# Moving input transposes between VectorE and TensorE in a fused attention and mixture-of-experts kernel

## The chip, the core and the metric

The kernel runs on one core of one Trainium2 chip. The metric is the device time of one execution in microseconds; the shown time is the median of three runs.

## The reference

The program computes one cross-attention layer and one mixture-of-experts layer over 4096 tokens of width 256, both with a residual. Cut to what matters:

```
x = x + xattn(ctx, layernorm(x), fside, fside, ...)      # 16 heads, 77 context rows
xn = layernorm(x)
probs = softmax(xn @ Wr)                                  # 9 experts
topk_w, topk_idx = top_k(probs, 2); topk_w /= sum(topk_w)
gate   = silu(xn @ Wg[e])                                 # 256 -> 704
hidden = gate * (xn @ Wu[e])
x = x + sum over the token's two experts e of topk_w[e] * (hidden @ Wd[e])   # 704 -> 256
```

## The kernel before

The program has two stages. The attention stage walks over 32 tiles of 128 tokens (i = 0 to 31 in the long loop that holds `scores`, `exponentials`, `weights_turn`, `values`). While it does so, the routing of each finished group of four tiles is worked out and every token is written with its weight into the list of each expert that it chose (`list_d` in DRAM).

The expert stage then walks over blocks of gathered tokens, all of one expert. A pair block has 256 tokens, a single block 128; a flex block is a single one whose two halves belong to two experts. There are 41 blocks, numbered j = 0 to 40: blocks 0 to 5 are early pairs (`EARLY = 6`), whose lists are complete before the last group is routed; from block 6 on a pair and a single alternate (blocks 6 to 35; the singles 9, 15, 21 and 27 are flex blocks, the other eleven are not), and blocks 36 to 40 are pairs. A further flex block, the rare one, has number 41 (`NBLK`) and is computed behind block 36 (`RARE_AT`) inside a `tc.If` on a count read from the routing; its products are skipped when the count is small, but its two additions to the output are always issued.

Engines run in the order in which the program lists their instructions; the kernel has switched to a manual order. For block j the loop issues:

- `fetch()`: SyncE loads the weights of block j+2 (`weights`, six transfers per expert); GpSimd gathers the token numbers of a later block (`tokens`, tile `ids`) and the rows of block j+2 (`inputs`, tile `yin`, an indirect DMA for each 128 rows; three `yin` buffers).
- the gate and up products. In a pair (`hidden_pair`) TensorE makes six chunks `pg`, f = 0 to 5, of 128 hidden units each (44 matmuls of 256 columns); ScalarE takes the silu of each (`sl`), VectorE multiplies (`hid`, L1249 and L1252). In a single (`hidden_one`) TensorE makes `psg`, `psu` and `psb` with the tokens as the stationary operand, ScalarE takes the silu, VectorE multiplies (`hs`, L1285 to L1290).
- the transposes of block j+1's rows from `yin` to `xT`, on VectorE: `turning` (L1215) has 16 instructions for a block, each of which turns a strip of 32 partitions in squares of 32 by 32. `advance(upcoming, 4)` issues four of them behind each chunk f = 1 to 4 of a pair; in a single all 16 stand behind the last `hs` multiplication. Blocks 0 and 1 are turned by TensorE instead (`turn`, L1228: four 128 by 128 transposes into PSUM tile `px`, and a copy by ScalarE, L1231).
- `down(j-1)`: TensorE multiplies the hidden units of the block before with `wd` (12 matmuls for each 128 tokens; 24 with half the columns for a flex block), VectorE scales by the routing weights (`co`, L1321).
- `adding(j-1)`: GpSimd adds the rows to the output by indirect DMA (L1353). Additions of different blocks may touch the same rows, so each waits until the ones before have landed; the two of a pair are declared independent.
- in a single, `hidden_turn`: TensorE turns `hs` (`ph`, six transposes), ScalarE and VectorE copy to `hid`.

During blocks 0 to 4, VectorE also finishes the routing of the last group and plans the later blocks; `pump()` issues up to six of these small instructions behind each chunk f of a pair. GpSimd writes the last group's list entries (L950, eight indirect DMAs) once VectorE has worked out their places (`r_pli`, L948).

At the head of the attention stage, two leftover pieces of a folded weight (`fill(left[...])`: TensorE products `pu`, L746, with one copy to `u` on ScalarE, L142, and one on VectorE, L140) are issued in steps i = 1 and i = 2, behind the third `scores`.

Of the kernel before, what the change touches and what calls it, by code (L numbers as in the profile page):

```python
# [21 lines left out]
def kernel(  # L22
# [231 lines left out]
    def scores(i, k):  # L254

        zT = zTs[i]
        h, n = banks[k]
        if k == 0:
            nmx[i] = stat.tile([P, H], F32, tag="mx", name=f"mx{i}")
        psc = pscs[k] = ps_sc.tile([P, TB], F32, tag=f"sc{k}", name=f"psc{i}_{k}")  # L260
        w = n * J + (E if h + n == H else 0)
        for c in range(C):
            nc.tensor.matmul(  # L263
                psc[:, :w], zT[:, c, :], g_sb[i // NS // GPB][:, c, h * J : h * J + w],
                start=(c == 0), stop=(c == C - 1),
            )
        nc.vector.tensor_reduce(  # L267
            nmx[i][:, h : h + n], psc[:, : n * J].rearrange("p (h j) -> p h j", h=n), AX.X,
            ALU.max, negate=True,
        )  # L270

    def exponentials(i, k):
        h, n = banks[k]
        if k == 0:
            exs[i] = pools["qpool"].tile([P, H, J], F32, tag="ex", name=f"ex{i}")
        for q in range(n):
            nc.scalar.activation(  # L277
                exs[i][:, h + q, :], pscs[k][:, q * J : (q + 1) * J], AF.Exp,
                bias=nmx[i][:, h + q : h + q + 1],
            )  # L280
# [75 lines left out]
    with ExitStack() as kvs:  # L356
# [436 lines left out]
        def fill(*what, new=mm_tile):  # L793

            for b, n in what:
                first_keys(b, n, new)
# [438 lines left out]
    def hidden_pair(j, also={}, upcoming=iter(())):  # L1235

        (w,), xT, hid = wgus.pop(j), xTs.pop(j), hids[j % 2]
        for f in range(NF + 1):
            pg = mm_tile(f"pg{j}_{f}").rearrange("p (g t) -> p g t", g=2)
            for g, at in enumerate((f * P, UP[f]) if f < NF else (f * P,)):  # L1240
                for c in range(C):
                    nc.tensor.matmul(  # L1242
                        pg[:, g, :], w[:, c, at : at + P], xT[:, c, :],
                        start=(c == 0), stop=(c == C - 1),
                    )
            sl = pools["spool"].tile([P, TS], F32, tag="sl", name=f"sl{j}_{f}")
            if f < NF:
                nc.scalar.activation(sl, pg[:, 0, :], AF.Silu)  # L1248
                nc.vector.tensor_tensor(hid[:, f, :], pg[:, 1, :], sl, ALU.mult)  # L1249
            else:  # L1250
                nc.scalar.activation(sl[64:128, :], pg[0:64, 0, :], AF.Silu)
                nc.vector.tensor_tensor(  # L1252
                    hid[64:128, NF, :], pg[64:128, 0, :], sl[64:128, :], ALU.mult
                )
            pump()
            if f:
                advance(upcoming, 4)
            for fn in also.get(f, ()):
                fn()
# [5 lines left out]
        n = P // len(of_experts)  # L1265
        return [slice(h * n, (h + 1) * n) for h in range(len(of_experts))]

    def hidden_one(j):


        ws, xT = wgus.pop(j), xTs.pop(j)
        hs = hss[j] = late["hs"] if j >= NBLK else pools["spool"].tile(
            [P, FF], F32, tag="hs", name=f"hs{j}", bufs=1
        )
        pgs = {}
        for k, (at, n) in (("g", (0, FA)), ("u", (FF + FB, FA)), ("b", (FA, 2 * FB))):
            pgs[k] = mm_tile(f"ps{k}{j}")
            for c in range(C):
                for w, rows in zip(ws, lanes(ws)):
                    nc.tensor.matmul(  # L1280
                        pgs[k][rows, :n], xT[:, c, rows], w[:, c, at : at + n],
                        start=(c == 0), stop=(c == C - 1),
                    )
        nc.scalar.activation(hs[:, :FA], pgs["g"], AF.Silu)
        nc.vector.tensor_tensor(hs[:, :FA], pgs["u"], hs[:, :FA], ALU.mult)  # L1285
        nc.scalar.activation(hs[:, FA:], pgs["b"][:, :FB], AF.Silu)
        nc.vector.tensor_tensor(
            hs[:, FA : NF * P], pgs["b"][:, FB + FT : 2 * FB], hs[:, FA : NF * P], ALU.mult
        )
        nc.vector.tensor_tensor(  # L1290
            hs[:, NF * P :], pgs["b"][:, FB : FB + FT], hs[:, NF * P :], ALU.mult
        )
# [139 lines left out]
    for i in range(N_SUB + 1):  # L1432
        g, s = divmod(i, NS)
        now_on = i < N_SUB
        q = g - 1

        if now_on:
            if i:
                scores(i, 0)
                exponentials(i, 0)  # L1440
            if i > 1:
                residual_stats(i - 2)
            if i:
                scores(i, 1)
            if 0 < i < N_SUB - 1:
                query(i + 1)
            if i:
                scores(i, 2)
        if i:
            if i < 3:  # L1450
                fill(left[i - 1])
            weights_turn(i - 1)
            weights_copy(i - 1, 0)
            weights_copy(i - 1, 1)
        if i == 2:
            vsides.close()
        if now_on and i:
            exponentials(i, 1)
        if 0 < i < N_SUB - 1:
            query_turn(i + 1)  # L1460
        if now_on and i:
            exponentials(i, 2)
        if i:
            weights_copy(i - 1, 2)
        if now_on:
            queries_logits(i)
            if s == 1 and q > 0:
                ranks(q - 1)
            if i == (G_EARLY + 1) * NS + 2:
                early = early_blocks()  # L1470
                advance(early, 2)
        else:
            turn(0)
            advance(chosen)
            ranks(q - 1)
            residual_stats(i - 2)
        if i:
            values(i - 1)


        if now_on and s == 0:
            if g + 1 < NG:
                for k in range(NS):
                    query_stats(g + 1, k)
            if q > 0:
                advance(chosen)
        if now_on and s == 1:
            if g + 1 < NG:
                query_variance(g + 1)
            if q >= 0:  # L1490
                advance(residual(q))
                root(q)
            if g + 1 < NG:
                query_root(g + 1)
            nc.scalar.activation(junk, eps_t, AF.Exp)
            if q > 0:
                advance(places(q - 1))
        if now_on and s == 2:
            if g + 1 < NG:
                query_scale(g + 1)  # L1500
            if q >= 0:
                advance(logits(q))
                exponential(q)
                advance(normalised(q))
            if g + 2 < NG:
                load_x(g + 2)
        if early is not None:
            if advance(early, 7):
                early = None
                now[0] = -1  # L1510
                fetch()
        if now_on and s == 3 and q >= 0:
            chosen = choices(q)
            advance(chosen, 14)
        if now_on:
            attention_weights(i)
        if i:
            attended(i - 1)
        if i == BH * GPB * NS:
            halves[0].close()  # L1520
            open_experts()
# [12 lines left out]
    for j in range(LAST):  # L1534
        now[0] = j
        if j == EARLY:
            assert not rest
            open_late()
        fetch()
        if j == EARLY + 1:  # L1540
            count = nc.values_load(
                tabs["flex_total"][0:1, 0:1], min_val=0, max_val=2 * FLEX
            )
        if j == RARE_AT - 1:
            tokens(NBLK)
            inputs(NBLK)
        if j == RARE_AT:
            weights(NBLK)
            weights_upper(NBLK)
        upcoming = turning(j + 1) if j else iter(())  # L1550
        if blocks[j][0] == 2:
            hidden_pair(j, upcoming=upcoming)
        else:
            hidden_one(j)
        advance(upcoming)
        if j:
            split(j + 1)
            down(j - 1)
            for r in rounds_of(j - 1):
                adding(*r)  # L1560
        if blocks[j][0] == 1:
            hidden_turn(j)
        if j == RARE_AT:
            split(NBLK)

            with tc.If(count > 2 * (FLEX - RARE)):
                turn(NBLK)
                hidden_one(NBLK)
                hidden_turn(NBLK)
                down(NBLK)  # L1570
            for r in rounds_of(NBLK):
                adding(*r)

    hidden_pair(LAST, {1: [lambda: down(LAST - 1), lambda: adding(*rounds_of(LAST - 1)[0])]})
    down(LAST)
# [34 lines left out]
```

## Time and profile before

| | us |
|---|---|
| median of three runs | 919.2 (916.86 to 920.8) |
| the profiled execution | 920.17 |
| its span | 918.4 |
| TensorE busy in the span | 894.0 (97%) |
| VectorE busy | 609.5 (66%) |
| ScalarE busy | 315.4 (34%) |
| GpSimd busy | 316.0 (34%) |
| VectorE on transposes L1215, 624 instructions | 172.5 |

The page gives busy times of each engine, the span in 40 slices, the chain that ended last, and the costliest groups of instructions by line and tile. A timeline lists instructions in the order of time: start, duration, engine, line, operation, output tile, input tiles, shape, number of merged instructions, and in brackets how long the engine had been idle and what ended that. PE is TensorE's matmul, PEld its weight load, DVE is VectorE, ACT ScalarE, POOL GpSimd.

### The profile page before, as it was taken

What the parts mean: (1) busy time and instruction counts of PE and PEld (TensorE: products, weight loads), DVE (VectorE), ACT (ScalarE), POOL (GpSimd) and SP (SyncE); (2) the same over time, 40 slices, a digit from 0 to 9 for tenths busy, and PEclk for the clock granted to TensorE, in tenths of its full rate; (3) what the DMA queues carried; (4) which work ended last, traced back from release to release, by engine and by line L of the source; (5) the groups of instructions that cost most, each with busy time, mean ns of one, the idle gap of its engine ahead of it and who ended that gap; (6) DMA issues with size and microseconds to landing.
All of it is one profiled execution on the core that took longest, in us unless ns stands there. A gap on an engine that the chain in (4) does not pass through costs nothing. (4 is left out here: it accounts for less than half of the span.)

```text
span 918.4 us, 13855 instructions
## 1 busy us (share of the span) xinstructions
PE 894.0 (97%) x4164; PEld 682.8 (74%) x4164; DVE 609.5 (66%) x1934; ACT 315.4 (34%) x1016; POOL 316.0 (34%) x328
## 2 busy tenths in 40 slices
PE   8999999999999999997999999999999999999996
PEld 6646777777777767786887777777777777778885
DVE  4776688878788887656974656656656656666551
ACT  3556566575656556441111111111111111111110
POOL 3000002130504343165345435435435435444432
PEclk9999999999999999999999999999999999999998
DMA  7001010512202700455769779879779877779722
GB/s 263 2 20 43 24 46 24 47 33 38 69 24 48 234 24 25 118 155 134 212 163 293 214 220 311 225 214 313 225 220 305 235 219 217 219 229 318 226 34 24
DMA packets 110378, 137.94 MB, mean 150 GB/s; under 512 B 24663, under 2 KB 80287, under 8 KB 110304
## 3 DMA queue, kind: packets, MB, share of 16 engines
q1 hardware_dynamic: 92746, 119.66, 41.9%
q0 software_dynamic: 17344, 17.26, 11.1%
q8 instruction: 34, 0.56, 0.3%
q14 instruction: 40, 0.33, 0.2%
q10 hardware_dynamic: 214, 0.13, 0.0%
HBM read 119.48 MB, written 18.33 MB: 150 GB/s over the span
## 5 line engine op out<-in xcount | busy, mean ns | idle before, releaser
L1242 PE MATMUL pg<-xT,wgu 128*128 128x256 f32 x1144 | 255.2, 383 | 9.1 <-issue 8.0
L1242 PEld LDWEIGHTS pg<-xT,wgu 128*128 128x128 f32 x1144 | 216.6, 191 | 43.1 <-issue 11.3
L1215 DVE STREAM_TRANSPOSE xT<-yin 32x128 f32<-32x128 f32 (+1 forms) x624 | 172.5, 276 | 18.9 <-DMA yin<-y_d,ids 9.7
L1318 PE MATMUL po<-wd,hid 128*128 128x256 f32 (+1 forms) x804 | 180.8, 380 | 0.0
L1318 PEld LDWEIGHTS po<-wd,hid 128*128 128x128 f32 (+1 forms) x804 | 149.6, 187 | 28.3 <-issue 3.7
L1353 POOL DMA_INDIRECT out_dram<-co,ids x63 | 100.7, 1599 | 176.5 <-DVE co L1321 153.1
L277 ACT ACTIVATE ex<-psc,mx 128x77 f32<-128x77 f32 x512 | 124.2, 362 | 104.1 <-DVE mx L267 98.0
L950 POOL DMA_INDIRECT list_d<-r_entry,r_pli x64 | 68.6, 1073 | 250.7 <-issue 123.5
L336 PE MATMUL po<-u,aT 128*128 128x265 f32 x640 | 151.6, 391 | 0.3
L263 PE MATMUL psc<-g,zT 128*128 128x462 f32 (+1 forms) x384 | 139.2, 511 | 0.0
L336 PEld LDWEIGHTS po<-u,aT 128*128 128x128 f32 x640 | 118.7, 189 | 23.1 <-ACT aT L325 0.9
L1248 ACT ACTIVATE sl<-pg 128x256 f32<-128x256 f32 x130 | 49.7, 384 | 230.2 <-PE pg L1242 162.9
L263 PEld LDWEIGHTS psc<-g,zT 128*128 128x128 f32 x384 | 72.3, 189 | 58.2 <-issue 50.5
L1249 DVE TENSOR_TENSOR hid<-pg,sl 128x256 f32<-128x256 f32 x130 | 55.1, 424 | 85.5 <-ACT sl L1248 67.7
L1183 POOL DMA_INDIRECT yin<-y_d,ids x67 | 70.7, 1055 | 24.2 <-issue 19.4
L297 DVE TENSOR_REDUCE sm<-ex 128x16 f32<-128x1232 f32 x32 | 45.9, 1434 | 35.3 <-ACT ex L277 32.3
L267 DVE TENSOR_REDUCE mx<-psc 128x6 f32<-128x462 f32 (+1 forms) x96 | 55.7, 581 | 18.2 <-PE psc L263 13.9
L325 ACT COPY aT<-pa 128x512 f32<-128x512 f32 (+1 forms) x96 | 49.5, 554 | 24.2 <-PE pa L317 24.2
L1321 DVE TENSOR_SCALAR co<-po,ids 128x256 f32<-128x256 f32 x67 | 30.6, 481 | 35.5 <-PE po L1318 34.8
L317 PEld LDWEIGHTS pa<-ident,an 128*128 128x128 f32 x320 | 36.7, 141 | 8.1 <-PE po L336 1.4
L317 PE MATMUL pa<-ident,an 128*128 128x128 f32 x320 | 40.3, 273 | 1.0 <-DVE an L301 1.0
L1285 DVE TENSOR_TENSOR hs<-psu,hs 128x512 f32<-128x512 f32 x15 | 10.4, 692 | 46.4 <-PE psu L1280 46.4
(312 smaller groups left out, 784.6 us busy)
## 6 DMA issues: line engine op xcount, KB each, us to landing
wgu<-in_L_ffn_Wg_dram SPq DMA_DIRECT2D x41, 704.0 KB
wd<-in_L_ffn_Wd_dram SPq DMA_DIRECT2D x41, 640.0 KB
wgu<-in_L_ffn_Wu_dram SPq DMA_DIRECT2D x41, 512.0 KB
wgu<-in_L_ffn_Wu_dram SPq DMA_DIRECT2D x41, 128.0 KB
x<-in_x_dram SPq DMA_DIRECT2D x8, 512.0 KB
out_dram<-x SPq DMA_DIRECT2D x8, 512.0 KB
y_d<-y SPq DMA_DIRECT2D x8, 512.0 KB
w<-in_L_ffn_Wg_dram SPq DMA_DIRECT2D x5, 704.0 KB
```

What stands on the lines that cost most here:

```text
L263: nc.tensor.matmul(psc[:, :w], zT[:, c, :], g_sb[i // NS // GPB][:, c, h * J : h * J + w], start=(c == 0), stop=(c == C - 1),)
L267: nc.vector.tensor_reduce(nmx[i][:, h : h + n], psc[:, : n * J].rearrange("p (h j) -> p h j", h=n), AX.X, ALU.max, negate=True,)
L277: nc.scalar.activation(exs[i][:, h + q, :], pscs[k][:, q * J : (q + 1) * J], AF.Exp, bias=nmx[i][:, h + q : h + q + 1],)
L317: nc.tensor.transpose(pa[:, q * P : (q + 1) * P], ans[i][:, (k + q) * P : (k + q + 1) * P], ident)
L336: nc.tensor.matmul(po[:, :DE], aT[:, n, :], u_sb[b][:, n, :], start=(n == 0), stop=(n == KC - 1))
L950: i = nc.gpsimd.indirect_dma_start(out=list_d[:, :], out_offset=bass.IndirectOffsetOnAxis(ap=place_i[:, s : s + 1], axis=0), in_=entries[k ...
L1183: return nc.gpsimd.indirect_dma_start(out=dst, out_offset=None, in_=src, in_offset=bass.IndirectOffsetOnAxis(ap=offsets, axis=0), **kw,)
L1215: yield nc.vector.transpose(xT[q : q + Q].rearrange("p c (h t) -> p h c t", t=P)[:, :nh, :, a : a + Q], of(yins, j)[a : a + Q].rearrange(" ...
L1242: nc.tensor.matmul(pg[:, g, :], w[:, c, at : at + P], xT[:, c, :], start=(c == 0), stop=(c == C - 1),)
L1249: nc.vector.tensor_tensor(hid[:, f, :], pg[:, 1, :], sl, ALU.mult)
L1318: nc.tensor.matmul(po[rows, :D], hid[:, f, at], d[:, f, :], start=(f == 0), stop=(f == NF))
L1353: i = nc.gpsimd.indirect_dma_start(out=out_r, out_offset=bass.IndirectOffsetOnAxis(ap=rows_of(j, h, rows), axis=0), in_=cos[j][:, h, :], i ...
```

## The change

Five edits. (1) Blocks 2 to 6 are turned by TensorE (`turn`), between the gate and up products of block j (j = 1 to 5) and `down(j-1)`; VectorE turns blocks 7 to 40. (2) In a pair, VectorE's four groups of four transposes stand behind chunks f = 2 to 5 instead of f = 1 to 4. (3) In a single, eight of the sixteen stand ahead of the `hs` multiplication with the up product, the other eight remain behind the last `hs` multiplication. (4) The rare block's two additions no longer follow block 36 directly: one stands behind block 37's addition (that of block 36), one behind block 38's. (5) The two leftover fills in steps 1 and 2 stand behind the first `scores` and ahead of the first `exponentials`.

```
@@ hidden_pair
-            if f:
+            if f > 1:
                 advance(upcoming, 4)
@@ hidden_one
-    def hidden_one(j):
+    def hidden_one(j, upcoming=iter(())):
...
         nc.scalar.activation(hs[:, :FA], pgs["g"], AF.Silu)
+
+        advance(upcoming, 8)
         nc.vector.tensor_tensor(hs[:, :FA], pgs["u"], hs[:, :FA], ALU.mult)
@@ the attention loop
             if i:
                 scores(i, 0)
+                if i < 3:
+                    fill(left[i - 1])
                 exponentials(i, 0)
...
         if i:
-            if i < 3:
-                fill(left[i - 1])
             weights_turn(i - 1)
@@ the block loop
-        upcoming = turning(j + 1) if j else iter(())
+
+        upcoming = turning(j + 1) if j >= EARLY else iter(())
         if blocks[j][0] == 2:
             hidden_pair(j, upcoming=upcoming)
         else:
-            hidden_one(j)
+            hidden_one(j, upcoming)
+        if 0 < j < EARLY:
+            turn(j + 1)
         advance(upcoming)
...
-            for r in rounds_of(NBLK):
-                adding(*r)
+            rare = rounds_of(NBLK)
+        elif j > RARE_AT and rare:
+
+            adding(*rare.pop(0))
+    assert not rare
```

## The prediction

> **What bounds the kernel now.** I read the page's first part, TensorE's waits, the timeline around them, and the windows. TensorE fills the span:
>
> ```profile
> span 918.4 us, 13855 instructions
> ...
> PE 894.0 (97%) x4164; PEld 682.8 (74%) x4164; DVE 609.5 (66%) x1934; ACT 315.4 (34%) x1016; POOL 316.0 (34%) x328
> ```
>
> 24.4 us of the span are without a matmul, so only time in which TensorE idles, runs slowed or does avoidable work can be won. The timeline of TensorE shows the largest stretch of idling, in the early pairs:
>
> ```profile
> 409.33 5.34 PE L1318 MATMUL po<-wd,hid 128*128 128x256 f32 x24
> 418.02 10.56 PE L1242 MATMUL pg<-xT,wgu 128*128 128x256 f32 x40 [3.34 <-issue]
> ...
> 436.56 9.73 PE L1242 MATMUL pg<-xT,wgu 128*128 128x256 f32 x44 [1.72 <-issue]
> ...
> 452.41 9.73 PE L1242 MATMUL pg<-xT,wgu 128*128 128x256 f32 x44 [0.94 <-issue]
> ...
> 468.78 9.73 PE L1242 MATMUL pg<-xT,wgu 128*128 128x256 f32 x44 [1.46 <-issue]
> ...
> 483.54 9.66 PE L1242 MATMUL pg<-xT,wgu 128*128 128x256 f32 x44
> ```
>
> Blocks 2 to 5 each begin late. "issue" names no culprit, but VectorE's timeline does: its last transposes for block 2 end at 417.91, 0.11 us ahead of TensorE's restart, and the same holds for the next three. The first group had waited for the gather:
>
> ```profile
> 410.37 1.25 DVE L1215 STREAM_TRANSPOSE xT<-yin 32x128 f32<-32x128 f32 x4 [3.16 <-DMA yin<-y_d,ids]
> ...
> 416.65 1.26 DVE L1215 STREAM_TRANSPOSE xT<-yin 32x128 f32<-32x128 f32 x4
> ```
>
> The windows show a second price, the clock (last but two column):
>
> ```profile
> 414.70:418.02 3.32, 0.00 (x1) 0.04 (x1) 3.03 (x14) 0.00 (x0) 0.00 (x0) 1.00 1.07 344
> 418.02:422.00 3.98, 3.98 (x11) 3.22 (x12) 1.72 (x5) 0.38 (x1) 3.01 (x3) 0.57 0.64 203
> ```
>
> From 484 to 842 TensorE shows no idle, but VectorE is close behind it. A single-to-pair and a pair-to-single change, from the timelines of weight loads, TensorE and VectorE:
>
> ```profile
> 763.12 9.36 PEld L1242 LDWEIGHTS pg<-xT,wgu 128*128 128x128 f32 x44 [0.23 <-DVE xT L1215]
> ...
> 775.10 0.41 PEld L1280 LDWEIGHTS psg<-wgu,xT 128*128 128x128 f32 x2
> ```
> ```profile
> 762.31 0.82 PE L1301 MATMUL ph<-ident,hs 128*128 128x128 f32 x6
> 763.12 9.76 PE L1242 MATMUL pg<-xT,wgu 128*128 128x256 f32 x44
> 772.72 2.75 PE L1318 MATMUL po<-wd,hid 128*128 128x256 f32 x12
> 775.31 1.88 PE L1280 MATMUL psg<-wgu,xT 128*128 128x512 f32 x4
> ```
> ```profile
> 761.80 1.26 DVE L1215 STREAM_TRANSPOSE xT<-yin 32x128 f32<-32x128 f32 x4
> ...
> 772.93 0.99 DVE L1215 STREAM_TRANSPOSE xT<-yin 32x64 f32<-32x64 f32 x4
> 773.96 0.43 DVE L1252 TENSOR_TENSOR hid<-pg,sl 64x256 f32<-64x256 f32 x1
> ```
>
> Last, block 39 begins 0.58 us late because block 38's transposes on VectorE waited 4.36 us for a gather that stood on GpSimd's queue behind the rare additions (855.66 and 862.58):
>
> ```profile
> 868.88 1.25 DVE L1215 STREAM_TRANSPOSE xT<-yin 32x128 f32<-32x128 f32 x4 [4.36 <-DMA yin<-y_d,ids]
> ```
>
> **What the Trainium skill says.** "TensorE: Matmul & The Clock Gate", Part 1, says that about 3.4 us of idling halve the clock. The trace agrees: 0.57 in the 4 us behind the 3.34 us gap; behind 1.72, 0.94 and 1.46 us the windows show 1.00. The same page, Part 2, says that weight loads are pulled ahead of running matmuls. The trace agrees: the load at 775.10 leads its matmul by 0.21 us. "VectorE: DVE Perf Modes", The three transpose paths, puts one 128 by 128 bf16 transpose at 390 ns on TensorE and 311 ns on VectorE, there only in squares of 32; here, in f32, four of them take TensorE 0.44 us back to back (384.08 to 384.52) and VectorE 16 instructions of 302 ns, 4.8 us: the measurement decides. "DMA: Bandwidth & Descriptors", Two DMAs through the same engine are not ordered, says that only a completed semaphore orders two transfers; the second rare addition indeed starts 6.9 us behind the first.
>
> **Edit 1, blocks 2 to 6 on TensorE.** Loss now: from 409.33 to 483.54 there are 5 down products of 5.18, 4 hidden parts of 44 matmuls at 9.50 / 44 = 0.216 us (860.02 to 869.52), 9.50 each, and 0.14 for a count: 64.0. It took 74.2, so 10.2 are lost: 7.5 idle, 3.98 x 0.43 = 1.7 of clock, 1.0 of smaller things. Added: five times four transposes. Rows of before: 0.44 for four in a stream, 0.60 with the drain; I take 0.5, as the first waits for its operand, so 2.5 (2.2 to 3.0). ScalarE's copies (two rows, 601 ns) lie beside the down product of 5.18 that follows; without that cover each would cost 0.6. TensorE runs in order, so down(j-1) now stands behind the gather. For block 2 that landed at 410.37, so TensorE idles 1.04 from 409.33, short of a slowed clock (bounds 0 and 2). For blocks 3 to 6 the gathers have time: block 3's are issued at 408.46 and 409.84 and needed at about 425.8. Block 4's stand behind the eight list writes and block 0's additions. The list writes waited for VectorE (418.14, behind transposes that go); they now start near 412 and end at 422, the additions follow, the gathers come near 426 to 429, wanted at 441. Block 6's come after block 2's additions and its `ids`, near 454 to 456, wanted at 471. SyncE's weights stay tied to the end of block j-1's hidden part and land a block ahead. Sum: 10.2 - 1.0 - 2.5 = 6.7, less 0.1 for rounding up the refills: 6.6 gained (5.5 to 8).
>
> **Edit 3, eight transposes ahead of the up product.** Eleven ordinary singles are followed by a pair whose first weight load waits for `xT` (763.12, the last transpose ends 763.06). From `ph` to `po` is 10.41 us; six transposes at 0.117 (739.19 to 739.90 behind a flex block) and 9.50 are 10.20. So 0.1 to 0.22 each; I take 0.15: 1.6 gained (1.2 to 2.4). The eight lie in VectorE's idle time ahead of `psu`: the wait before the first `hs` product, L1285, sums to 46.4 us over 15 blocks, 3.1 each, and eight cost 2.5. They need block j+1's gather; those of 744.39 and 745.78 are needed near 753. If one is late, the `hs` product queues behind it; `down(j-1)`, 5.18, covers that.
>
> **Edit 2, the last group one chunk later.** It now comes behind L1252: 773.96 + 0.46 + 0.98 = 775.40, load at +0.06 = 775.46 instead of 775.10. Matmuls then start about 0.1 to 0.2 behind the load, at 775.6 instead of 775.31: 0.3 lost. This needs a short down product ahead, one of 128 tokens (2.59). That is so in 14 pairs, 8 to 34. Six lie between two ordinary singles: 6 x 0.3 = 1.8 (0.15 to 0.5 each). Next to a flex block TensorE starts 2.69 to 2.74 behind the hidden part for its own reasons: 8 x 0.05 = 0.4. Block 36 also has one in front: there VectorE's co and two small operations slip from 844.24 to about 844.7, and TensorE's restart behind the branch, which names VectorE (1.07 idle, 845.27), slips with it: 0.5. Together 2.7 lost (1.5 to 4.5). Pairs followed by pairs have 5.18 and hide it.
>
> **Edit 4, rare additions.** GpSimd then gathers block 39 near 848 instead of 864.44: block 39 starts at 869.52 + 5.18 = 874.70 instead of 875.44, 0.7 gained. The price is in other places of the queue: the first addition waits for block 36's to land (7 to 9 us, as 846.61 to 855.66), with block 40's gathers behind it near 870, as late as now (871.00). The second waits near 879 and has landed before block 38's at 888.57. The end is set by down(40) at 910.05 in any case. 0.
>
> **Edit 5, the fills.** The transposes `pz` wait 1.10 for the copy on ScalarE at 70.37. With the copy earlier, `z` on VectorE, now behind its own copy, is ready near 70.3 instead of 69.95: 0.3 gained (0 to 0.6). Step 2 has no idle: 0.
>
> **Sum:** 6.6 + 1.6 - 2.7 + 0.7 + 0.3 = 6.5. On the profiled execution 920.17 - 6.5 = 913.7; that run lies 1.0 above the median, so 919.2 - 6.5 = 912.7.
>
> **Rivals.** (A) As summed: 912.7, own range 910.5 to 914.5, chance 0.53. (B) The late group is absorbed and edit 3 is worth its upper bound: 6.5 + 2 + 0.8 = 9.3, and block 2's gather is a little earlier: 909. For it, no single wait is long; against it, the load cannot precede its operand. 0.20. (C) Loss at the 14 places is 0.3 throughout plus the branch and edit 3 gives its lower bound: 6.6 + 1.2 + 1.0 - 4.7 = 4.1, block 2's gather another microsecond late: 916. 0.22. (D) Slower: TensorE, in order, stands ahead of the down product for a late gather. Price each as at block 2 now: 3.3 idle and 1.7 of clock, 5.0. From 6.5 in all, two such places, it decides; three give 919.2 - 6.5 + 15 = 927.7. For it, gathers follow additions and list writes on one queue, and one landed 5.9 us behind its issue; against it, the slack of 12 us or more at blocks 3 to 6. 0.04. (E) The edit does not act: the transposes could have landed behind the down product; the order of TensorE's instructions shows four `px` ahead of `po` in blocks 1 to 5, so 919, 0.01.
>
> **How the numbers follow.** The range 908.5 to 916.5 takes in A, most of B and C, and a spread of runs like 916.9 to 920.8. Half a per cent, 4.6 us, is about what can be told from no change: faster is below 914.6. That is A, B and a small part of C, 0.75; slower by as much is most of D, 0.03; 0.22 between.
>
> **What would show it.** Right: no idle in front of blocks 3 to 6, about 1 us ahead of block 2's `px`, a clock of 1.00 from 412 to 484, block 6 starting 6 to 7 us earlier; no weight load behind `xT` in single-to-pair; one 0.2 to 0.4 late in six pair-to-single changes; block 39 without a wait. Wrong: a `px` waiting over 2 us for `yin`, or pair-to-single losses over 0.6 us each.

## The result and the profile after

The changed kernel takes 910.01 us, the median of six runs (908.26 to 911.39), beside 919.67 us for the kernel before (six runs, 916.86 to 920.8). The ratio is 0.9898, with a 95% interval of 0.988 to 0.9916: 9.7 us less, where 6.5 were forecast. 910.0 lies inside the range, between cases A (912.7) and B (909), nearer to B, and just below A's own range (910.5 to 914.5).

The first lines of the page of the changed kernel:

```profile
span 906.6 us, 13816 instructions
...
PE 890.6 (98%) x4184; PEld 684.0 (75%) x4184; DVE 588.2 (65%) x1854; ACT 317.8 (35%) x1021; POOL 315.9 (35%) x328
```

TensorE has 20 matmuls more (5 blocks, 4 transposes each), VectorE 80 instructions less, and 16.0 us of the span are without a matmul in place of 24.4. The timeline of TensorE in the early pairs of the changed kernel:

```profile
407.59 0.30 PE L1228 MATMUL px<-ident,yin 128*128 128x128 f32 x1
408.18 0.55 PE L1228 MATMUL px<-ident,yin 128*128 128x128 f32 x3 [0.28 <-DMA yin<-y_d,ids]
408.56 5.34 PE L1320 MATMUL po<-wd,hid 128*128 128x256 f32 x24
413.74 8.80 PE L1242 MATMUL pg<-xT,wgu 128*128 128x256 f32 x40
...
429.08 9.66 PE L1242 MATMUL pg<-xT,wgu 128*128 128x256 f32 x44
438.58 0.60 PE L1228 MATMUL px<-ident,yin 128*128 128x128 f32 x4
439.01 5.35 PE L1320 MATMUL po<-wd,hid 128*128 128x256 f32 x24
444.20 9.66 PE L1242 MATMUL pg<-xT,wgu 128*128 128x256 f32 x44
...
459.31 9.66 PE L1242 MATMUL pg<-xT,wgu 128*128 128x256 f32 x44
...
474.43 9.66 PE L1242 MATMUL pg<-xT,wgu 128*128 128x256 f32 x44
```

Every block follows the last without a bracket: 15.12, 15.11 and 15.12 us from block 3 on. The four `px` take 0.43 to 0.44 us (438.58 to 439.01), and only block 2's wait for the gather. The bracket shows 0.28 us of that wait, but it is longer: the first `px` starts 1.24 us behind the last row of matmuls (406.35), where block 3's starts 0.95 behind its row (422.51 to 423.46), and the four take 0.97 (407.59 to 408.56). Together 0.8 us are lost there. The windows from one block's start to the next show a clock (last but two column) of 1.00:

```profile
413.74:429.08 15.34, 15.34 (x75) 13.53 (x74) 6.93 (x20) 2.88 (x7) 9.67 (x10) 1.00 0.44 119
429.08:444.20 15.12, 15.12 (x74) 13.31 (x73) 9.59 (x44) 2.88 (x7) 8.83 (x7) 1.00 0.84 200
```

Later, a single-to-pair and a pair-to-single change of the changed kernel, on TensorE:

```profile
545.03 0.82 PE L1303 MATMUL ph<-ident,hs 128*128 128x128 f32 x6
545.69 9.66 PE L1242 MATMUL pg<-xT,wgu 128*128 128x256 f32 x44
555.19 2.75 PE L1320 MATMUL po<-wd,hid 128*128 128x256 f32 x12
557.97 1.95 PE L1280 MATMUL psg<-wgu,xT 128*128 128x512 f32 x4
```

The pair starts 0.66 us behind `ph` where it took 0.81, and its hidden part lasts 9.50 us (545.69 to 555.19) where it lasted 9.60 (763.12 to 772.72). The single starts 2.78 us behind the down product where it took 2.59. Its first weight load leads its matmul by only 0.03 us, where it led by 0.21, and VectorE's timeline says for what it waits:

```profile
557.94 0.30 PEld L1280 LDWEIGHTS psg<-wgu,xT 128*128 128x128 f32 x2 [0.40 <-issue]
```
```profile
556.41 0.43 DVE L1252 TENSOR_TENSOR hid<-pg,sl 64x256 f32<-64x256 f32 x1
556.87 0.99 DVE L1215 STREAM_TRANSPOSE xT<-yin 32x64 f32<-32x64 f32 x4
```

The last four transposes end at 557.86, the load follows 0.08 later and the matmul 0.03 behind that. Last, GpSimd's queue behind the branch:

```profile
838.80 1.04 POOL L1183 DMA_INDIRECT yin<-y_d,ids  x1 [0.30 <-issue]
840.15 1.02 POOL L1183 DMA_INDIRECT yin<-y_d,ids  x1 [0.31 <-issue]
847.79 1.62 POOL L1355 DMA_INDIRECT out_dram<-co,ids  x1 [6.63 <-DVE co L1323]
...
856.57 1.56 POOL L1355 DMA_INDIRECT out_dram<-co_r,alone  x1 [5.07 <-DMA out_dram<-co,ids]
...
869.17 1.56 POOL L1355 DMA_INDIRECT out_dram<-co_r,alone  x1 [2.99 <-issue]
877.14 1.56 POOL L1355 DMA_INDIRECT out_dram<-co,ids  x1 [6.41 <-DVE co L1323]
```

Block 39's gathers now stand ahead of both rare additions, and block 39 starts 14.67 us behind block 38 in place of 15.42.

To compare kernels, the timeline of TensorE is cut at the same instructions in each: A from the first `pwq` (the start of its four transposes behind the long `pk`) to the first values product; B from the end of block 1's hidden part to the start of block 6; C from there to the end of block 36's hidden part; D from there to the start of block 37 (the branch); E from block 38's start to block 39's. The end of a hidden part is taken as the start of the next instruction in the list, so in the first profile of the changed kernel 0.29 us of block 2's wait lie ahead of B. "P to S" is the time from the end of a pair's hidden part to a single between ordinary singles, "S to P" from `ph` to the down product behind the next pair's hidden part.

| us | A | B | C | D | E | P to S | S to P |
|---|---|---|---|---|---|---|---|
| before | 53.14 | 74.21 | 357.91 | 3.82 | 15.42 | 2.59 | 10.41 |
| before, second profile | 53.14 | 72.85 | 357.91 | 3.82 | 14.68 | 2.59 | 10.41 |
| changed | 52.85 | 66.84 | 356.30 | 3.48 | 14.67 | 2.78 | 10.15 |
| changed, second profile | 52.85 | 67.16 | 356.54 | 3.47 | 14.67 | 2.78 | 10.15 |
| edit 1 alone | 53.14 | 67.05 | 358.70 | 3.16 | 15.31 | 2.59 | 10.41 |
| edit 2 alone | 53.15 | 81.33 | 359.45 | 4.29 | 14.68 | 2.78 | 10.41 |
| edit 3 alone | 53.13 | 72.91 | 354.58 | 3.89 | 14.96 | 2.59 | 10.15 |
| edit 4 alone | 53.13 | 70.80 | 358.65 | 3.82 | 14.67 | 2.59 | 10.41 |
| changed, edit 2 undone | 52.86 | 67.08 | 354.62 | 3.16 | 14.68 | 2.59 | 10.15 |
| the same, second profile | 52.85 | 66.96 | 354.65 | 3.16 | 14.68 | 2.59 | 10.15 |

Means of two profiles each give B -6.5, C -1.5, D -0.35, E -0.38, A -0.29: 9.0 us in all, beside 9.66 between the medians. The two profiles first shown differ by 11.8 us of span; 1.76 of that lie ahead of A (`pwq` starts at 18.19 and 16.43), where the start in other profiles lies anywhere from 15.7 to 20.5, whatever the kernel. This part is not the change's.

B of the kernel before is not a fixed number. Edits 3 and 4 leave its early blocks as they were, so the table holds four profiles of them: 74.21, 72.85, 72.91 and 70.80. With edit 1 it is 66.84 to 67.16 in five profiles. The gain in B is thus 3.6 to 7.4 us, depending on the two profiles that are compared, and 5.7 between the means of the four and of the five; the profile that the prediction started from is the one with the largest loss.

### The profile page after: what moved, and what is told of

The parts are those of the page before. It is cut to its first block, busy times and chain, and to the rows that moved or that the text cites. A ratio compares the mean times of both kernels' runs of the same rounds, so it can differ in the third digit from the quotient of the medians.

```text
span 906.6 us, 13816 instructions
## 1 busy us (share of the span) xinstructions
PE 890.6 (98%) x4184; PEld 684.0 (75%) x4184; DVE 588.2 (65%) x1854; ACT 317.8 (35%) x1021; POOL 315.9 (35%) x328
## 5 line engine op out<-in xcount | busy, mean ns | idle before, releaser
L1242 PE MATMUL pg<-xT,wgu 128*128 128x256 f32 x1144 | 251.7, 379 | 0.7 <-DVE xT L1215 0.7
L1215 DVE STREAM_TRANSPOSE xT<-yin 32x128 f32<-32x128 f32 (+1 forms) x544 | 148.4, 273 | 14.2 <-DMA yin<-y_d,ids 5.4
L950 POOL DMA_INDIRECT list_d<-r_entry,r_pli x64 | 69.0, 1078 | 247.3 <-issue 119.7
L301 DVE TENSOR_TENSOR an<-ex,rs 128x1024 f32<-128x1024 f32 x32 | 39.2, 1224 | 1.1
```

The costliest lines, as they stand in the source:

```text
L950: i = nc.gpsimd.indirect_dma_start(out=list_d[:, :], out_offset=bass.IndirectOffsetOnAxis(ap=place_i[:, s : s + 1], axis=0), in_=entries[k ...
L1215: yield nc.vector.transpose(xT[q : q + Q].rearrange("p c (h t) -> p h c t", t=P)[:, :nh, :, a : a + Q], of(yins, j)[a : a + Q].rearrange(" ...
L1242: nc.tensor.matmul(pg[:, g, :], w[:, c, at : at + P], xT[:, c, :], start=(c == 0), stop=(c == C - 1),)
```

## The experiments

The theory was the prediction's sum, edit by edit; the rivals were that the early pairs' gain is really that of block 2 alone, that the place of the transposes in TensorE's order doesn't matter, and that edit 2 is harmless or even needed. Single runs give a profile to read; their times differ by several us from run to run of the same kernel.

**Edit 1 alone.**

```
+        upcoming = turning(j + 1) if j >= EARLY else iter(())
...
+        if 0 < j < EARLY:
+            turn(j + 1)
```

> The kernel before with edit 1 alone (blocks 2 to 6 turned by TensorE). Theory: most of the gain is here, because TensorE no longer waits at the starts of blocks 2 to 5 and its clock stays up. From the end of block 1's hidden part to the start of block 6: 67.1 us as in the changed kernel (74.2 before), the rest of the trace as before; time 7 us (0.77%) below the kernel before, 5.5 to 8. Rival (the edits act together, VectorE being relieved over the whole run): under 5 us here, and the remainder only when edits 2 and 3 are added.

Measured: 913.37 us (22 runs) beside 917.21 (27 runs of the kernel before), ratio 0.9956 (0.9939 to 0.9973). B is 67.05, so the early pairs' gain comes from this edit. But the medians differ by 3.8 us only (2.5 to 5.6 by the interval), less than the 5.5 to 8 that were expected and less than the 5.8 to 7.2 by which B is shorter than in the two profiles of the kernel before. By the time alone the rival, under 5 us, would hold; B, as short here as in the changed kernel, speaks against it. Part of C went the other way (one change of a pair to a single took 3.30 us instead of 2.59; such a single outlier also stands in edit 4 alone, 3.23, and in the second profile of the changed kernel, 2.99). What remains of the difference is open. A candidate that was not tested is the variation of the kernel before: its 27 runs lie between 914.63 us, at a mean clock of 0.997, and 924.48, at 0.991, so many of them may have lost less in B than the first profile, whose time of 920.17 is 3.0 above their median. D fell to 3.16, which no term of the sum had for this edit.

**The changed kernel with edit 2 undone.** `if f > 1:` is `if f:` again.

> The changed kernel with edit 2 undone (VectorE's groups again behind chunks 1 to 4 of a pair). Theory: edit 2 is a loss, 0.19 us at each of the six changes from a pair to a single between two ordinary singles, 1.1 in all; the single-to-pair changes keep their gain from edit 3. Each of those pair-to-single changes goes back from 2.78 to 2.59 us; time 1.1 us (0.13%) below the changed kernel, so about 908.9. Rival (edit 2 was needed: with the group one chunk earlier VectorE waits for gathers ahead of a multiplication): up to 2 us slower than the changed kernel, with waits of VectorE for yin over 1 us behind chunk 1.

Measured: 908.65 us (six runs) beside the same 917.21, ratio 0.9898 (0.9865 to 0.993). C is 1.7 us and D 0.3 us below the changed kernel, together nearly twice the 1.1 expected, and the early pairs are no worse. The time doesn't show it here: the ratio is that of the changed kernel, 0.9898.

**Edit 2 alone.** `if f:` becomes `if f > 1:` in the kernel before.

> The kernel before with edit 2 alone (groups behind chunks 2 to 5). Theory: pair-to-single changes between two ordinary singles grow from 2.59 to 2.78 us, six times, single-to-pair stays at 10.41 us from ph to po, nothing else moves but the restart behind the branch, which could come up to 0.5 later: 1 to 2 us more from block 6 to block 37. Rival (later groups relieve VectorE): the single-to-pair changes shrink to 10.2 too, and the stretch gets shorter.

Measured: one run, 929.28 us. P to S, S to P and the branch came as expected (C is 1.5 longer, D 0.5), but the expectation that nothing else moves was wrong: B is 81.33, 7 to 8.5 longer than in the two profiles of the kernel before. The timelines of TensorE and of VectorE in this kernel:

```profile
440.35 12.07 PE L1242 MATMUL pg<-xT,wgu 128*128 128x256 f32 x44 [5.69 <-issue]
452.26 5.34 PE L1318 MATMUL po<-wd,hid 128*128 128x256 f32 x24
460.15 9.73 PE L1242 MATMUL pg<-xT,wgu 128*128 128x256 f32 x44 [2.55 <-issue]
```
```profile
435.68 1.25 DVE L1215 STREAM_TRANSPOSE xT<-yin 32x128 f32<-32x128 f32 x4
436.95 0.43 DVE L1252 TENSOR_TENSOR hid<-pg,sl 64x256 f32<-64x256 f32 x1
...
438.99 1.26 DVE L1215 STREAM_TRANSPOSE xT<-yin 32x128 f32<-32x128 f32 x4
```

Between the third and the fourth group VectorE has the last `hid` and six routing instructions, so block 3's `xT` is complete only at 440.25. Edit 2 puts the last group behind the routing work of the early pairs. Not all of the 7 to 8.5 us is due to that: block 2's silus came 1.4 to 4.5 us late here, a hold-up that the kernel before has too and that is described below. Block 4 is the cleaner place: block 3's silus are on time, and block 4 still starts 7.90 us behind block 3's hidden part, where 6.28 was the time before. Edit 1 takes these transposes from VectorE, so in the changed kernel only the price in C and D is left. The edits do not add up one by one. The prediction rightly charged nothing for edit 2 in the early pairs, but its reason, that a pair behind a pair has 5.18 us and hides the late group, does not hold there: edit 1 is what makes it harmless.

**Edit 3 alone.** `advance(upcoming, 8)` ahead of the up product in the kernel before.

> The kernel before with edit 3 alone (eight transposes ahead of the multiplication with the up product in a single). Theory: ph to po at the eleven single-to-pair changes falls from 10.41 to 10.16 us, 2.75 us in all, and pair-to-single stays at 2.59; block 6 to the end of block 36's hidden part takes 2.75 us less. Rival (the shorter change comes from edit 2 or from both together): 10.41 stays or falls by less than 0.1.

Measured: one run, 915.54 us; C is 354.58, 3.33 shorter, where 2.75 was expected. Eleven changes at 0.26 are 2.86, and four behind flex blocks, 10.36 to 10.25, another 0.44, which the expectation left out: together 3.30.

**Edit 4 alone.** The rare additions as in the changed kernel.

> The kernel before with edit 4 alone (the rare block's additions behind blocks 37 and 38). Theory: block 39's gather leaves GpSimd's queue some 15 us earlier, so block 38 to block 39 takes 14.7 instead of 15.4 us, and nothing is given back at the end: from block 39's start to the last down product 29.4, from there to the end of the span 13.5. Its early pairs and its stretch from block 6 to 36 are those of the kernel before (74 and 357.9), a second look at how far these vary. Rival (the deferred additions hold up the last ones): the time from the last down product to the end grows by 0.5 us or more.

Measured: one run, 915.95 us; E is 14.67, and nothing is given back at the end (29.35 and 13.57 us). But E is 14.68 as well in the second profile of the kernel before, with edit 2 alone and in the run below that turns block 2 alone, and 14.96 with edit 3 alone. B, expected at 74, is 70.80, though this edit touches nothing in the early pairs. Without edit 4 the gather is sometimes late and sometimes not, so the edit is worth 0 to 0.75 us; the 0.7 of the prediction is its upper end.

**Block 2 alone turned by TensorE**, the other edits undone.

```
-        upcoming = turning(j + 1) if j else iter(())
+        upcoming = turning(j + 1) if j > 1 else iter(())
...
+        if j == 1:
+            turn(j + 1)
```

> The kernel before with block 2 alone turned by TensorE, blocks 3 to 6 left to VectorE. Theory: block 2's lateness is 3.3 us of idling and 1.7 of clock, against 0.3 of waiting and 0.44 for the transposes, so block 1's end to block 3's start falls from 27.2 to about 22.6 us less whatever VectorE still holds up at block 3; blocks 3 to 5 stay 1.0 to 1.7 us late each. From block 1's hidden end to block 6: 69 to 71 us, against 74.2 before and 67 with edit 1. Rival (VectorE's arrears carry over from block 2 to the others): blocks 3 to 5 start on time too, 67.5.

Measured: one run, 921.64 us, and B is 72.26, above the 69 to 71 expected and inside what the kernel before shows. Block 2 is on time (5.62 us behind block 1's hidden part), but block 3 starts 3.39 us late, with the clock down (44 matmuls in 11.42 us for 9.66), and blocks 4 and 5 are 0.58 and 1.34 late. The lateness moved on; one block was no remedy in this profile. The timeline of ScalarE shows where it came from this time:

```profile
423.20 0.38 ACT L1248 ACTIVATE sl<-pg 128x256 f32<-128x256 f32 x1 [1.34 <-PE pg L1242]
427.32 0.38 ACT L1248 ACTIVATE sl<-pg 128x256 f32<-128x256 f32 x1 [3.73 <-PE pg L1242]
431.63 0.38 ACT L1248 ACTIVATE sl<-pg 128x256 f32<-128x256 f32 x1 [3.93 <-remote]
433.15 0.38 ACT L1248 ACTIVATE sl<-pg 128x256 f32<-128x256 f32 x1 [1.14 <-PE po L1318]
```

TensorE finishes a chunk every 1.73 us without a pause, yet from the third on the silus come 2.4 to 5.2 us behind their chunk ("remote" means that the profile knows no releaser). VectorE's `hid` and the transposes queued behind it are late by as much.

**The transposes behind the down product.** In the changed kernel, `turn(j + 1)` stands behind `down(j - 1)`.

> The changed kernel with TensorE's transposes of blocks 2 to 6 behind down(j-1) instead of ahead of it. Theory: the down product of 5.18 us is what hides ScalarE's copy; with it gone each of blocks 2 to 6 waits for the drain of the transposes and a copy of 0.60: 0.7 to 0.9 each, 3.5 to 4.5 us more from block 1's hidden end to block 6 (about 71). Block 2 loses its wait for the gather, 0.3, in turn. Rival (the gain of edit 1 is VectorE's relief alone, the place doesn't matter): 67 to 67.5.

Measured: one run, 921.4 us, B is 75.18, more than the 71 expected. The timeline of TensorE:

```profile
433.69 0.60 PE L1228 MATMUL px<-ident,yin 128*128 128x128 f32 x4
437.56 11.45 PE L1242 MATMUL pg<-xT,wgu 128*128 128x256 f32 x44 [3.27 <-ACT xT L1231]
448.85 5.34 PE L1320 MATMUL po<-wd,hid 128*128 128x256 f32 x24
454.03 0.60 PE L1228 MATMUL px<-ident,yin 128*128 128x128 f32 x4
455.30 9.76 PE L1242 MATMUL pg<-xT,wgu 128*128 128x256 f32 x44 [0.68 <-ACT xT L1231]
```

Without the down product as cover, each block waits 0.68 us for ScalarE's copy and takes 0.94 longer (16.06 us from block 4's start to block 5's, for 15.12): 0.16 go to the end of the transposes, which no down product covers any more, and 0.10 are lost within the hidden part. The prediction priced the copy alone, at 0.6. So the place of the transposes matters. Block 3 pays more: its copy ran at 436.92, though `px` was done at 434.29, and behind the idle time its 44 matmuls took 11.45 us. That part, most of what exceeds the expectation, is again ScalarE being held up around 427 to 437.

**All sixteen transposes ahead of the up product**, in the changed kernel.

> The changed kernel with all sixteen transposes of a single ahead of the multiplication with the up product. Theory: that multiplication comes up to 2.5 us later, but its result is needed by the ph transposes only behind down(j-1), 5.18 us: ph to po stays at 10.15 and block 6 to the end of block 36's hidden part at 356.3 within 0.3. Rival (VectorE's idle time ahead of the up product, 3.1 us on average, is the limit): TensorE waits for hs at each of the eleven ordinary singles, 0.5 us or more each, or for banks that the late multiplication holds.

Measured: one run, 913.36 us. S to P stays at 10.15, so eight are enough. C is 357.21, 0.7 to 0.9 longer than in the changed kernel and outside the 0.3 expected; nearly all of it is one wait of TensorE for `hs`, 0.7 us at one single, while the others show none.

**The late writes left out.** The kernel before without the eight writes of the last group's list entries (L950): this group's tokens then do not go to the experts.

```
-            for s in range(NS):
+            for s in range(NS if g < TOK // TB - 1 else 0):
```

> The kernel before without the eight writes of the last group's list entries, so that this group's tokens do not go to the experts. Theory (these writes, or the traffic behind them, cause the stop of ScalarE near 424 to 430): no silu of block 2 comes over 0.5 us late, and the stretch from the end of block 1's hidden part to block 6 takes 69 to 72 us. Rival (the stop has another cause): a silu of blocks 2 or 3 still comes 2 to 4 us late.

Measured: one run, B is 71.66. ScalarE's timelines of block 2, first the kernel before, then this one:

```profile
425.16 0.38 ACT L1248 ACTIVATE sl<-pg 128x256 f32<-128x256 f32 x1 [1.34 <-issue]
429.50 0.38 ACT L1248 ACTIVATE sl<-pg 128x256 f32<-128x256 f32 x1 [3.96 <-PE pc_late L969]
432.36 0.38 ACT L1248 ACTIVATE sl<-pg 128x256 f32<-128x256 f32 x1 [2.48 <-PE po L1318]
```
```profile
427.57 0.38 ACT L1248 ACTIVATE sl<-pg 128x256 f32<-128x256 f32 x1 [1.34 <-PE pg L1242]
429.30 0.38 ACT L1248 ACTIVATE sl<-pg 128x256 f32<-128x256 f32 x1 [1.34 <-PE pg L1242]
431.03 0.38 ACT L1248 ACTIVATE sl<-pg 128x256 f32<-128x256 f32 x1 [1.34 <-PE pg L1242]
432.11 0.38 ACT L1251 ACTIVATE sl<-pg 64x256 f32<-64x256 f32 x1 [0.70 <-PE pg L1242]
```

Block 2's silus are on time here. Of the thirteen profiles with the writes, twelve have a silu of block 2 that is 2.3 us late or more; the first profile of the changed kernel has none. That points to the writes, but one profile without them can't show it, and block 1's first silu comes 6.1 us behind its chunk in this kernel too (409.74), just after the writes of the group before were issued (the last at 403.17). By what path such writes could hold ScalarE is open.

**Both versions once more, on one chip, and the kernel before.**

> The changed kernel once more, timed on the same chip as the version that leaves edit 2 out. Theory (edit 2 costs 0.26 us at each of six places and about 0.3 us at the branch, in all 1.9 us): this one is 1.5 to 2.2 us slower than without_2_again; b6 to the end of block 36's hidden part 356.3 us, branch 3.5 us. Rival (edit 2 is needed in the early pairs and gives there what it costs later): the two are within 0.5 us. Theory on the early pairs (a stop of ScalarE of some 4 us near 424 to 430, seen in all profiles but the first of this kernel, is a matter of the execution and not of the kernel): a second profile is likely to show a silu that comes 2 to 4 us late in block 2, and the stretch from the end of block 1's hidden part to block 6 stays at 66.8 to 67.3 us, as the down product covers the copy. Rival (the changed order avoids the stop): no silu late by over 0.5 us.

> The changed kernel with edit 2 undone (groups behind chunks 1 to 4 again). Theory: 1.5 to 2.2 us faster than the changed kernel on the same chip; ordinary single to pair to single 2.59 us in place of 2.78, b6 to the end of block 36's hidden part 354.6 us, branch 3.2 us. Rival: within 0.5 us of it.

> The kernel before, profiled once more. Theory (the early stretch varies with a stop of ScalarE whose place varies): from the end of block 1's hidden part to block 6 between 70 and 75 us, and not 74.2 again; the rest, block 6 to the end of block 36's hidden part, 357.9 us again and the branch 3.8 us again. Rival (all of the kernel's stretches repeat to 0.2 us): 74.2 us.

Measured: changed 911.43 us (seven runs, ratio to before 0.9922, 0.9893 to 0.995), with edit 2 undone 907.65 (five runs, 0.9874, 0.9852 to 0.9896), before 919.76 (twelve runs). The medians differ by 3.8 us, more than the 1.5 to 2.2 expected and than the 2.2 that C and D explain; the two intervals overlap by a little, while in both pairs of profiles C is 1.7 to 1.9 and D 0.3 shorter. The version without edit 2 has the lowest median of all. The second profile of the changed kernel has the hold-up, too (a silu of block 2 about 2.3 us late, the copy at 431.24), and B grows by only 0.3, as the down product covers most of the copy's lateness: block 3 starts 5.56 us behind the start of the down product, where 5.18 is the pace. The order takes most of the lateness off TensorE's path, it doesn't prevent it. The kernel before had B 72.85 in its second profile, with C and D the same to 0.01.

## Why the prediction was right and where it was wrong

**What bounds the kernel: right.** The kernel was on TensorE before and is after; the idle and slow stretch in the early pairs was the largest thing to win.

**Edit 1: right as to mechanism; as to size, right for the profile it was worked out from.** 6.6 were forecast. Against the two profiles of the kernel before, the two of the changed kernel give 5.7 to 7.4, 6.5 in the mean; against all four profiles with the same early blocks it is 5.7 in the mean, and timed alone the edit gave 3.8. The 10.2 us of loss were taken from one execution, and others lost up to 3.4 us less, for which no term of the sum allowed. The terms added lay close: the `px` cost 0.44 and not 0.5, and block 2's gather cost 0.8 in the first profile of the changed kernel and less or nothing in the others, where 1.04 was forecast. The last list writes were issued from 416.67 to 426.71, later than the 412 to 422 forecast, but the slack at blocks 3 to 6 sufficed, so rival D (TensorE standing in order behind a late gather) didn't come about.

The clock stays up, 1.00 in all windows here, and no long gap is left. "TensorE: Matmul & The Clock Gate", Part 1, on which the clock's term rested, names about 3.4 us of idling. The slowed 11.42 and 11.45 us behind gaps of 3.39 and 3.27 us are near to that. But the clock also fell behind shorter gaps, of 2.41 us with edit 2 alone (417.91) and of 2.50 in the second profile of the kernel before (415.54): six and seven matmuls in a row started 0.43 us apart there, where 0.22 is the pace. Behind a gap of 2.55 with edit 2 alone (460.15) it stayed at 1.00. So here the measurement decides: 3.4 us is no safe limit, and the length of the gap alone doesn't tell.

**Edit 3: mechanism right, size too small; this term failed.** 11 x 0.15 = 1.6 was taken from 0.1 to 0.22. Measured were 11 x 0.26 and 0.44 more behind flex blocks, 3.3, above the bound of 2.4. The prediction's floor for `ph` came from a flex place of the kernel before (739.19 to 739.90, 0.71), and that place was itself waiting: the changed kernel needs 0.65 or 0.66 there. And it took 9.50 us for the pair's hidden part from a place without a late load, but then took 0.15 instead of the whole difference; behind a late load the hidden part itself lasts 9.60.

**Edit 2: mechanism right, size too large.** Forecast were 6 x 0.3 + 8 x 0.05 in C and 0.5 at the branch. Measured: P to S 0.19 and, from `psg` to `psu`, 1.79 for 1.72, so 0.26 at each of six places, 1.6; nothing next to flex blocks (2.69 and 2.74 as before); 0.3 at the branch. Half of the 0.8 too much is the term next to flex blocks. At the six places the start was overrated, as the matmul follows a late load by 0.03 and not by 0.1 to 0.2, and the slower matmuls behind it were left out.

**The branch: not foreseen.** D was to grow by 0.5 and shrank by 0.35. Edit 1 alone takes it from 3.82 to 3.16, edit 2 puts 0.3 back. In the kernel before TensorE's restart follows an event of VectorE's at the join, in those with edit 1 and without edit 2 it precedes VectorE's next two instructions; in the changed kernel it waits for the late transposes:

```profile
832.69 1.26 DVE L1215 STREAM_TRANSPOSE xT<-yin 32x128 f32<-32x128 f32 x4
833.99 0.48 DVE L1323 TENSOR_SCALAR co<-po,ids 128x256 f32<-128x256 f32 x1
...
834.21 1.10 PE L1242 MATMUL pg<-xT,wgu 128*128 128x256 f32 x4 [0.72 <-DVE xT L1215]
```

Why an edit to blocks 2 to 6 shortens the way through a branch at block 36 is open; with block 2 alone turned by TensorE, D is 3.45, between the two.

**Edits 4 and 5.** Edit 5 gave 0.29 (forecast 0.3), in all six profiles that have it. Edit 4 gave 0 to 0.75.

**The sum.** The forecast total was 6.5, the measured parts make 9.0. The difference is C (forecast +0.6, measured -1.5) and D (+0.5 and -0.35), less 0.3 at E. So B's reasons were half right: edit 3 above its upper bound, edit 2 partly absorbed. That the time still fell into the range is owed in part to its width of 8 us: edit 3 was worth twice its term, the branch had the wrong sign, and edit 1's term rests on one profile with a large loss.

## What to carry to other kernels

When an engine that isn't the bound sits between a late input and the bound, a small amount of work on the bound (here 0.44 us a block) can be cheaper than the wait, if what follows it (here a down product of 5.18 us) covers the last copy. Where such a wait varies from one execution to the next, take its size from several profiles. Price a wait at a floor from a place that itself doesn't wait, and take the whole difference. An edit whose worst harm another one hides (edit 2 beside edit 1) is worth undoing by itself: here that gave the lower median where both were timed on one chip (907.65 and 911.43 us), and the shorter stretches C and D in every profile.

## What was not expected of the hardware

- While the last eight list writes and the two additions behind them were under way, what waited for TensorE on ScalarE came 2.3 to 5.6 us late in twelve of thirteen profiles (427.32, 431.63 and 433.15 above), while TensorE ran on. In the one profile without these writes it didn't; the cause is not shown. In the kernel before, VectorE's transposes queue behind it, which may be why its B varies from 70.80 to 74.21; in the changed kernel the down product hides most of it.
- Gaps of 2.41 and 2.50 us in TensorE's work were followed by about 3 us at half the pace, and one of 2.55 us was not.
- A late weight load cost time twice at a change from a single to a pair: 0.16 us at the start and 0.10 more within the 44 matmuls that follow it.
